# One attention layer's edges: the first batch's expert sums divided anew between VectorE and GpSimd, the last batch's splits spread over rounds, its last projections and statistics reordered

## The chip, the cores and the metric

The kernel runs on one core of a Trainium2 chip. The metric is the device time of one execution in microseconds (us), lower is better. TensorE is called PE, VectorE DVE, ScalarE ACT and GpSimd POOL, as in the profile.

## The reference, cut to what matters

Two transformer layers with a layer norm behind every sublayer, on x of 8 batches x 512 tokens x 512 features, all in fp32:

```python
x = L0_attn_x
x = _layernorm(x + _L0_attn_ref(x, ...))   # 16 heads, causal
x = _layernorm(x + _L0_ffn_ref(x, ...))    # 8 experts, the 2 best of each token, weighted
x = _layernorm(x + _L1_attn_ref(x, ...))   # 8 query heads on 2 key/value heads
x = _layernorm(x + _L1_ffn_ref(x, ...))    # integer weights times a scale, SiLU-gated
```

The change lies in the third line and at its borders. In short, that line is

```python
def _L1_attn_ref(x, norm_scale, split_scale, Wq, Wk, Wv, Wo):
    nrm = jnp.linalg.norm(x, axis=-1, keepdims=True) * d ** (-0.5)
    h = norm_scale * x / (nrm + EPS) * split_scale
    q, k, v = h @ Wq.T, h @ Wk.T, h @ Wv.T          # by heads
    attn = softmax(q k / sqrt(64)); out = attn v
    return x + out @ Wo.T
```

## The kernel before, in words

The 512 tokens of a batch b are held as `xs[b]`, 128 partitions x 4 row blocks (t = 0 to 3) x 512 features. Layer 1's attention (`Attention1`) runs over the 8 batches in turn. Within a batch there are 4 head pairs g, and for each pair 4 key blocks kt: 16 units. A round i of 8 takes two units, so that an even round has kt 0 and 1 of a pair and an odd round kt 2 and 3. In `batches`, a round issues, in this order:

- `score` of its two units: two matmuls each on PE ("sc", two tiles of two PSUM banks each), and the exponential on ACT (L1582) into one of four buffers "p";
- `add` (L1590) of the units of the round before, on DVE: the running "total" over key blocks, one addition after an even round, two after an odd one;
- the round's further pieces of work, from the list `todo[i]` that `plan` (L1616) makes;
- `product` (L1601) of the units of the round before, on PE ("av"), and, when these ended a head pair, `normalise` (L1606): the row sums "rs" on PE (L1609) from the total, their copy to SBUF on ACT (L931), the reciprocal on DVE (L1612), the product with "av" into "aoT" on DVE (L1613), and a running sum for a later validity test on POOL (L934).

The further pieces are: `query` (L1498), the projection of the next head pair's queries; `project` (L1544), the output projection of one row block of the batch before (`project_groups`, one matmul for each of the 4 head pairs) with `residual` (L1554), which adds x on DVE (L1557) and takes the statistics of the layer norm (L1561, L1562; for the last row block also two small POOL operations, L1565 and L1566); `norm` (L1568), which applies it; and the preparation of the next batch. That preparation (`Combine`, L655) gathers the two expert results of each row block from DRAM by indirect DMA on POOL's queue (`fetch`, L673, eight gathers "yr"), adds them to x with their weights, either on DVE with two fused operations (`add`, L680, then `stat`) or on POOL with four operations (`sum`, L689 and L690, with `stat` issued separately), takes statistics on DVE (`stat`, L694, L695), computes deviations on POOL (L701 to L703), norms on DVE (L710 to L714, "xn"), and turns the result with PE (`turn`, L1477) for `key`, `value` and `query`. In batch 0 the preparation is that of batch 1, and its gathers begin with the stage, since the gathered rows are then complete; POOL does the sums of three row blocks, DVE those of one. In the other batches DVE does all four.

In the last batch there is no next batch to prepare. Instead it makes the input of layer 1's feed-forward part for batch 0: `split` (L1012), for each of 4 feature blocks c, turns x on PE into a PSUM tile "ps_xT" (L1022), rounds it on ACT to "x_high" (L1023) and takes the remainder on DVE as "x_low" (L1024).

After the last round the last total, products and row sums follow, then the output projection of batch 7 into four PSUM tiles `banks`, and its statistics. Then `IntegerFfn.run` (L1026) begins: for each batch 11 chunks c of the hidden width. A chunk's gate and up matmuls (L1055, "ps_g" and "ps_u") are followed by SiLU on ACT (L1058), a product on DVE (L1060, "hT"), its rounding on ACT (L1063) and its remainder on DVE (L1064). The down matmuls (L1069, "ps_f") of a chunk come after the gate and up matmuls of the next. Weights come as integers by DMA from SP's queue into one slot (L980), are converted on DVE (L994), and their largest magnitude is watched on DVE (L926) for the validity test.

What sets the order: in layer 1's attention, PE, DVE, ACT and POOL run their instructions in the order of the code (`in_order`, L1523), each engine waiting where an input is missing. In the feed-forward part the framework's planner orders the instructions by its own estimate of when each is ready, with the order of the code as priority; low-priority ones fill gaps. PSUM has 8 banks: in the attention, two for the tag "mm" (queries, projections, splits, row sums), four for "sc" and two for "av". A tile of a tag takes a buffer that is free, and waits for one if none is. The feed-forward part opens its own PSUM tiles over all of them, and its first matmul waits for the last readers of the banks that it takes.

Of the kernel before, what the change touches and what calls it, by code (L numbers as in the profile page):

```python
# [18 lines left out]
P = 128  # L19
NB = 8  # L20
S = 512
D = 512
NT = S // P
ND = D // P
# [48 lines left out]
class Env:  # L73
# [19 lines left out]
    def open_stream(self, ctx, batches, **kw):  # L93

        resident = ctx.enter_context(self.tc.tile_pool(name=f"resident{batches[0]}", bufs=1, **kw))
        for b in batches:
            self.xs[b] = resident.tile([P, NT, D], F32, tag=f"x{b}", name=f"x_{b}")
# [904 lines left out]
class IntegerFfn:  # L1002
# [9 lines left out]
    def split(self, b, c, ps):  # L1012


        nc = self.nc
        if c == 0:
            pool = self.work if b % 2 else self.rows
            self.halves[b] = [pool.tile([P, ND, S], F32R, tag=f"rows{i}", name=f"x3_{part}")
                              for i, part in enumerate(("high", "low"))]
        high, low = self.halves[b]  # L1020
        for t in range(NT):
            nc.tensor.transpose(ps[:, ts(t, P)], self.env.xs[b][:, t, ts(c, P)], self.env.ident)  # L1022
        nc.scalar.copy(high[:, c, :], ps)  # L1023
        nc.vector.tensor_tensor(low[:, c, :], ps, high[:, c, :].bitcast(F32), ALU.subtract)  # L1024
# [420 lines left out]
class Attention1:  # L1445
# [80 lines left out]
    def batches(self, work, p_sc, p_av, weights, split):  # L1526
        env, nc, guard, state, HD = self.env, self.nc, self.guard, self.state, self.HD
        xs = env.xs
# [15 lines left out]
        def project(b, t):  # L1544
            ps = self.mm([P, D], "ps_o1")
            project_groups(b, t, ps, range(ND))
            residual(b, t, ps)

        def project_groups(b, t, ps, groups):
            for c in groups:  # L1550
                nc.tensor.matmul(ps, lhsT=state[b]["aoT"][:, c, ts(t, P)], rhs=w_out[:, c, :],  # L1551
                                 start=c == 0, stop=c == ND - 1)

        def residual(b, t, ps):  # L1554
            st = state[b]
            x = xs[b][:, t, :]
            nc.vector.scalar_tensor_tensor(x, x, st["scale"][t], ps, ALU.mult, ALU.add)  # L1557
            if t == 0:
                st["stats"] = small.tile([P, NT, 6], F32, name="stats1")
                st["mv"] = small.tile([P, NT, 2], F32, name="mv1")  # L1560
            nc.vector.bn_stats(out=st["stats"][:, t, :], in_=x)  # L1561
            nc.vector.bn_aggr(out=st["mv"][:, t, :], in_=st["stats"][:, t, :])  # L1562
            if t == NT - 1:
                st["rstd"] = rstd = small.tile([P, NT], F32, name="rstd1")
                nc.gpsimd.tensor_scalar(rstd, st["mv"][:, :, 1], LN_EPS, None, ALU.add)  # L1565
                nc.gpsimd.tensor_tensor(rstd, rstd, env.neg_half, ALU.pow)  # L1566

        def norm(b):  # L1568
            st = state.pop(b)
            for t in range(NT):  # L1570
                x = xs[b][:, t, :]
                nc.vector.tensor_scalar(x, x, st["mv"][:, t, 0:1], st["rstd"][:, t : t + 1], ALU.subtract, ALU.mult)
# [21 lines left out]
        def product(b, g, kt, p):  # L1594
            st = state[b]
            if b and (g, kt) == (0, 0):
                st["aoT"] = work.tile([P, ND, S], F32, tag="aoT", name="aoT1", bufs=2)
            if kt == 0:
                st["av"] = p_av.tile([P, S], F32, tag="av", name="av1")
            for j in range(2):  # L1600
                nc.tensor.matmul(st["av"][HD * j : HD * (j + 1), :], lhsT=st["v"][:, kt, HD * j : HD * (j + 1)],  # L1601
                                 rhs=p[:, j, :], start=kt == 0, stop=kt == NT - 1)
            if kt == NT - 1:
                return lambda total=st["total"], av=st["av"]: normalise(b, g, total, av)
# [11 lines left out]
        def plan(b):  # L1616


            todo = [[] for _ in range(ND * NT // 2)]
            here = pieces.pop(b)  # L1620
            first, final = b == 0, b == NB - 1
            then = None if final else self.prepare(b + 1)
            if not final:
                pieces[b + 1] = then
                todo[0] += [lambda t=t: then["fetch"](t) for t in range(NT)]
            for g, i in zip((1, 2, 3), (1, 3, 5) if first else (0, 1, 5) if final else (0, 1, 3)):
                todo[i].append(lambda g=g: here["query"](g))
            if b:
                for t, i in enumerate((2, 3, 4, 7) if final else (2, 3, 4, 5)):
                    todo[i].append(lambda t=t: project(b - 1, t))  # L1630
                if not final:
                    todo[6].append(lambda: norm(b - 1))
            if final:
                for c, i in enumerate((4, 6, 6, 6)):
                    todo[i].append(lambda c=c: split(0, c, self.mm([P, S], "ps_xT")))
            else:
                if first:

                    for t, i in ((1, 1), (2, 2), (3, 3)):
                        todo[i].append(lambda t=t: then["sum"](t))  # L1640
                        todo[i + 1].append(lambda t=t: then["stat"](t))
                for t, i in ((0, 2),) if first else ((0, 2), (1, 2), (2, 3), (3, 4)):
                    todo[i].append(lambda t=t: then["add"](t))
                todo[4].append(then["deviations"])

                todo[5].insert(0, then["norm"])
                todo[6] += [lambda c=c: then["turn"](c) for c in range(ND)]
                todo[6].append(then["key"])
                todo[7] += [then["value"], lambda: then["query"](0)]
            for i in (7,) if first else (1, 7):  # L1650
                todo[i] += [weights.convert, lambda: weights.load(work, 2, weights.FIRST)]
            return todo

        last = []
        for b in range(NB):
            for i, thunks in enumerate(plan(b)):
# [6 lines left out]
                sums = [product(*unit) for unit in last]  # L1663
# [3 lines left out]
        for unit in last:  # L1667
            add(*unit)
        sums = [product(*unit) for unit in last]
        sums[-1]()  # L1670

        b = NB - 1
        banks = [self.mm([P, D], "ps_o1") for _ in range(2)]
        banks += [p_sc.tile([P, 2, S], F32, tag="sc", name="ps_o1")[:, 0, :] for _ in range(2)]
        for t in range(NT):
            project_groups(b, t, banks[t], range(ND - 1))
        norm(b - 1)
        for t in range(NT):
            project_groups(b, t, banks[t], (ND - 1,))
            residual(b, t, banks[t])  # L1680
        return lambda: norm(b)


# [346 lines left out]
```

## Time and profile before

| | us |
|---|---|
| three runs | 2298.08, 2293.88, 2297.77 |
| median | 2297.77 |
| profiled execution, time | 2295.71 |
| profiled execution, span of its instructions | 2293.9 |
| PE busy | 2240.5 (98%) |
| DVE busy | 1245.0 (54%) |
| ACT busy | 648.2 (28%) |
| POOL busy | 501.6 (22%) |
| layer 1's attention, first score to last projection | 1189.5 to 1772.3 |

Times inside the kernel are counted from the start of the span. The span is about 1.8 us shorter than the time of the same execution, and the profiled execution lies between the lowest and the highest of the three runs. In the profile a matmul of 512 columns in fp32 appears as two records, and ends of matmuls are modelled, so records overlap slightly.

### The profile page before, as it was taken

The page shows a single profiled execution, that of the slowest core. Times are in us where ns is not written, and L with a number is a line of the kernel's source. Part 1 is how long each engine was busy: PE and PEld are TensorE (multiplying, and loading weights), DVE is VectorE, ACT ScalarE, POOL GpSimd, SP SyncE. Part 2 cuts the span into 40 slices and gives each one's busy share as a digit, 9 for nine tenths or more (in the row PEclk, how much of TensorE's full clock was granted, in tenths as well). Part 3 has the DMA queues.
Part 4 walks back from the last instruction along what each step waited for, and adds up shares of the span by engine and source line. Part 5 has one row for each costly group of instructions (what it writes and reads, how often), then busy time and mean ns, then how long its engine had stood idle before and what let it go on. Part 6 is the DMA issues. An engine that isn't in the chain of part 4 may idle for free.

```text
span 2293.9 us, 24187 instructions
## 1 busy us (share of the span) xinstructions
PE 2240.5 (98%) x9430; PEld 1154.8 (50%) x9430; DVE 1245.0 (54%) x1974; ACT 648.2 (28%) x937; POOL 501.6 (22%) x493
## 2 busy tenths in 40 slices
PE   9999999999999999999998999999998999999997
PEld 3344444444444444444443334443343878888876
DVE  3457575666668432242216877777667544444443
ACT  2332323323324221111223323333332322222222
POOL 2231323413224231131125122321211000000000
PEclk9999999999999999999999999999999999999999
DMA  8010110101112234332233011100100100000000
GB/s 289 19 56 1 55 33 23 56 7 49 54 38 84 92 115 146 93 120 91 87 127 94 10 55 56 55 29 17 37 1 23 42 19 19 19 19 19 19 19 20
DMA packets 58444, 126.63 MB, mean 55 GB/s; under 512 B 6210, under 2 KB 6210, under 8 KB 58322
## 3 DMA queue, kind: packets, MB, share of 16 engines
q1 hardware_dynamic: 47040, 89.32, 11.1%
q0 software_dynamic: 10560, 34.61, 5.2%
q8 instruction: 77, 1.26, 0.2%
q10 hardware_dynamic: 722, 1.07, 0.1%
q14 instruction: 45, 0.37, 0.1%
HBM read 89.59 MB, written 35.39 MB: 54 GB/s over the span
## 4 chain that ended last, share of the span: by engine, by line
PE 76%; issue 8%; DVE 7%; DMA 4%; POOL 4%; ACT 2%; POOLq 0%; SPq 0%; ACTq 0%; DVEq 0%
PE ps_f L1069 7%; PE ps_g L1055 6%; PE ps_u L1055 6%; PE ps_gu L845 5%; PE ps_o L1216 5%; PE ps_o L1551 5%; PE av L1601 5%; PE sc L1579 4%; PE ps_q L1503 4%; PE ps_q L1200 4%; PE ps_k L1208 4%; PE ps_v L1193 4%; PE av L1288 3%; PE sc L1264 3%; PE ps_y L862 2%
## 5 line engine op out<-in xcount | busy, mean ns | idle before, releaser
L845 PE MATMUL ps_gu<-experts,xrT 128*128 128x512 f32 (+1 forms) x520 | 248.6, 601 | 0.0
L1268 ACT ACTIVATE p<-sc 128x2048 f32<-128x2048 f32 (+1 forms) x96 | 152.9, 1593 | 189.0 <-PE sc L1264 182.1
L1273 POOL TENSOR_SCALAR_AFFINE_SELECT p<-p 128x512 f32<-128x512 f32 x128 | 92.1, 734 | 380.1 <-ACT p L1268 376.6
L1060 DVE SCALAR_TENSOR_TENSOR hT<-ps_u,vec,sg 128x512 f32<-128x512 f32 x88 | 65.8, 748 | 201.4 <-PE ps_u L1055 201.4
L1069 PE MATMUL ps_f<-ffn_w,h_half 128*128 128x512 f32 x672 | 169.4, 392 | 1.1 <-DVE h_half L1064 1.1
L934 POOL TENSOR_TENSOR g_total<-g_total,r_inv 128x512 f32<-128x512 f32 x64 | 89.7, 1402 | 361.4 <-DVE r_inv L1612 286.2
L1612 DVE RECIPROCAL r_inv<-r_inv 128x512 f32<-128x512 f32 x32 | 106.8, 3339 | 105.4 <-ACT r_inv L931 105.4
L1582 ACT ACTIVATE p<-sc 128x1024 f32<-128x1024 f32 x128 | 124.1, 1021 | 130.3 <-PE sc L1579 119.7
L1296 DVE TENSOR_TENSOR p<-p 128x1536 f32<-128x1536 f32 (+2 forms) x96 | 129.3, 1346 | 38.5 <-POOL p L1273 21.5
L1055 PE MATMUL ps_g<-x_high,ffn_w 128*128 128x512 f32 x352 | 141.5, 402 | 3.0 <-DVE x L1557 3.0
L1069 PEld LDWEIGHTS ps_f<-ffn_w,h_half 128*128 128x128 f32 x672 | 124.5, 188 | 33.7 <-DVE h_half L1064 7.2
L848 DVE TENSOR_TENSOR h<-ps_gu,h 128x256 f32<-128x256 f32 x67 | 28.4, 424 | 205.2 <-ACT h L847 205.2
L1055 PE MATMUL ps_g<-x_low,ffn_w 128*128 128x512 f32 x352 | 139.4, 396 | 0.0
L1055 PE MATMUL ps_u<-x_high,ffn_w 128*128 128x512 f32 x352 | 139.2, 395 | 0.0
L1055 PE MATMUL ps_u<-x_low,ffn_w 128*128 128x512 f32 x352 | 139.2, 395 | 0.0
L1579 PE MATMUL sc<-qT,kT 64*128 64x512 f32 x512 | 127.9, 618 | 1.0 <-ACT qT L1505 0.7
L862 PE MATMUL ps_y<-experts,hT 128*128 128x512 f32 (+1 forms) x272 | 127.9, 592 | 0.5 <-ACT hT L856 0.5
L1200 PE MATMUL ps_q<-experts 128*128 128x512 f32 x256 | 120.4, 611 | 4.4 <-DMA experts<-in_xT 4.4
L845 PEld LDWEIGHTS ps_gu<-experts,xrT 128*128 128x128 f32 x520 | 89.6, 192 | 68.0 <-issue 68.0
L1601 PE MATMUL av<-p,v 128*64 128x512 f32 x512 | 123.8, 605 | 0.0
L1193 PE MATMUL ps_v<-experts 128*128 128x512 f32 x256 | 116.3, 602 | 2.4 <-DVE v L1195 2.4
L1208 PE MATMUL ps_k<-experts 128*128 128x512 f32 x256 | 117.5, 602 | 0.2 <-ACT r_inv L931 0.2
(256 smaller groups left out, 3544.5 us busy)
## 6 DMA issues: line engine op xcount, KB each, us to landing
results<-y SPq DMA_DIRECT2D x68, 256.0 KB
x<-in_x SPq DMA_DIRECT2D x8, 1024.0 KB
experts<-in_gate_up SPq DMA_DIRECT2D x8, 1024.0 KB
rows<-x SPq DMA_DIRECT2D x32, 256.0 KB
x<-rows SPq DMA_DIRECT2D x8, 1024.0 KB
experts<-in_xT SPq DMA_DIRECT2D x7, 1024.0 KB
out<-x SPq DMA_DIRECT2D x28, 256.0 KB
ffn_i<-in_wq_ffn SPq DMA_DIRECT2D x11, 512.0 KB
```

The source lines that it names most:

```text
L845: mm = nc.tensor.matmul(ps, lhsT=xT[:, c, :], rhs=self.weights(i, c), start=c == 0, stop=c == ND - 1)
L862: self.nc.tensor.matmul(ps, lhsT=hT[:, c, :], rhs=self.weights(i, ND + c), start=c == 0, stop=c == self.NI - 1)
L1055: nc.tensor.matmul(ps, lhsT=w[:, ts(dc, P)], rhs=x[:, dc, :], start=(dc, i) == (0, 0), stop=(dc, i) == (ND - 1, 1))
L1069: self.nc.tensor.matmul(os[t], lhsT=h[:, ts(t, P)], rhs=self.weights(2 * NHID + c), start=(c, i) == (0, 0), stop=(c, i) == (NHID - 1, 1))
L1193: nc.tensor.matmul(ps, lhsT=xts[b][:, c, ts(t, P)], rhs=wv[:, c, :], start=c == 0, stop=c == ND - 1)
L1200: nc.tensor.matmul(ps, lhsT=wq[:, g, ts(c, P)], rhs=xts[b][:, c, :], start=c == 0, stop=c == ND - 1)
L1208: nc.tensor.matmul(ps, lhsT=wk[:, g, ts(c, P)], rhs=xts[b][:, c, :], start=c == 0, stop=c == ND - 1)
L1268: nc.scalar.activation(p, sc[:, :, :width], AF.Exp, scale=scale)
L1296: nc.vector.tensor_tensor(total[:, :, P * kt :], total[:, :, P * kt :], p[:, :, at : at + w], ALU.add)
L1579: nc.tensor.matmul(sc[:, j, :], lhsT=st["kT"][hs, ts(kt, P)], rhs=st["qT"][g][hs, :], start=True, stop=True)
L1582: nc.scalar.activation(p, sc, AF.Exp, scale=scale)
L1601: nc.tensor.matmul(st["av"][HD * j : HD * (j + 1), :], lhsT=st["v"][:, kt, HD * j : HD * (j + 1)], rhs=p[:, j, :], start=kt == 0, stop=kt ...
```

## The change

There are four edits.

1. In batch 0, POOL sums row blocks 2 and 3 (in rounds 1 and 2, their statistics on DVE two rounds later instead of one) and DVE adds row blocks 0 and 1 (in rounds 1 and 2). Before, POOL summed 1, 2 and 3 (rounds 1, 2 and 3) and DVE added block 0 in round 2. The gathers keep their order.
2. In the last batch the four splits are issued in rounds 0, 2, 4 and 6 instead of 4, 6, 6 and 6.
3. After the last round, the projection of row block 0 of batch 7 into the first bank, for three of the four head pairs, is issued ahead of the last row sums. The second bank is taken after them.
4. `statistics` is a function of its own. `project` still calls it right behind `residual`; at the end of the last batch the four residuals are issued first and the four row blocks' statistics behind them.

```diff
@@ project
             residual(b, t, ps)
+            statistics(b, t)
...
             nc.vector.scalar_tensor_tensor(x, x, st["scale"][t], ps, ALU.mult, ALU.add)
+
+        def statistics(b, t):
+            st = state[b]
+            x = xs[b][:, t, :]
             if t == 0:
...
@@ plan
             if final:
-                for c, i in enumerate((4, 6, 6, 6)):
+                for c, i in enumerate((0, 2, 4, 6)):
                     todo[i].append(lambda c=c: split(0, c, self.mm([P, S], "ps_xT")))
             else:
                 if first:
-                    for t, i in ((1, 1), (2, 2), (3, 3)):
+                    for t, i in ((2, 1), (3, 2)):
                         todo[i].append(lambda t=t: then["sum"](t))
-                        todo[i + 1].append(lambda t=t: then["stat"](t))
-                for t, i in ((0, 2),) if first else ((0, 2), (1, 2), (2, 3), (3, 4)):
+                        todo[i + 2].append(lambda t=t: then["stat"](t))
+                for t, i in ((0, 1), (1, 2)) if first else ((0, 2), (1, 2), (2, 3), (3, 4)):
                     todo[i].append(lambda t=t: then["add"](t))
                 todo[4].append(then["deviations"])
...
@@ batches, after the last round
         sums = [product(*unit) for unit in last]
+
+        b = NB - 1
+        banks = [self.mm([P, D], "ps_o1")]
+        project_groups(b, 0, banks[0], range(ND - 1))
         sums[-1]()
-
-        b = NB - 1
-        banks = [self.mm([P, D], "ps_o1") for _ in range(2)]
+        banks.append(self.mm([P, D], "ps_o1"))
         banks += [p_sc.tile([P, 2, S], F32, tag="sc", name="ps_o1")[:, 0, :] for _ in range(2)]
-        for t in range(NT):
+        for t in range(1, NT):
             project_groups(b, t, banks[t], range(ND - 1))
         norm(b - 1)
         for t in range(NT):
             project_groups(b, t, banks[t], (ND - 1,))
             residual(b, t, banks[t])
+        for t in range(NT):
+            statistics(b, t)
         return lambda: norm(b)
```

## The prediction

> **What bounds the kernel now.** I read the page first, then the timelines of PE, DVE and POOL through the layer-1 attention (1187 to 1786 us), then the busy time and granted clock in 1 us stretches around each gap of PE.
>
> ```profile
> PE 2240.5 (98%) x9430; PEld 1154.8 (50%) x9430; DVE 1245.0 (54%) x1974; ACT 648.2 (28%) x937; POOL 501.6 (22%) x493
> ```
>
> PE is busy 98% of the span, so the time is PE's work plus its gaps. Its timeline has four large gaps in this stage, and each touches the change. First batch, rounds 2 to 5 (start, length, engine, work, [idle before <- releaser]):
>
> ```profile
> 1202.99 1.03 PE L1609 MATMUL rs<-total,ones 128*64 128x512 f32 x4
> ...
> 1213.28 1.94 PE L1601 MATMUL av<-p,v 128*64 128x512 f32 x8
> 1220.09 1.97 PE L1609 MATMUL rs<-total,ones 128*64 128x512 f32 x4 [4.87 <-DVE total L1590]
> ```
>
> The row sums of head pair 1 (rs) start 4.87 us after PE was free, on DVE's total. DVE's timeline says why that total is late:
>
> ```profile
> 1205.88 0.69 DVE L694 BATCH_NORM_STATS2 stats<-x 128x6 f32<-128x512 f32 x1 [9.26 <-POOL x L690]
> ...
> 1206.70 2.58 DVE L680 SCALAR_TENSOR_TENSOR x<-yr,r_weights,x 128x512 f32<-128x512 f32 x2
> ...
> 1216.64 3.39 DVE L1590 TENSOR_TENSOR total<-total,p 128x1024 f32<-128x1024 f32 x2
> ```
>
> DVE stood 9.26 us waiting for GpSimd's first sum; recip, the next totals and rs stood behind it. The idle also halves the clock (each stretch: length, busy time of PE, PEld, DVE, ACT and POOL, then PEclk, DMA share, GB/s):
>
> ```profile
> 1220.00:1221.00 1.00, 0.91 (x3) 0.29 (x4) 0.04 (x1) 0.00 (x0) 1.00 (x1) 0.50 0.00 0
> ...
> 1222.00:1223.00 1.00, 1.00 (x4) 0.50 (x4) 0.15 (x1) 0.69 (x2) 0.82 (x1) 0.50 0.00 0
> ```
>
> From rs to the next products PE needs 8.13 us (1220.09 to 1228.22); the same steps take 6.5 later (1333.06 to 1339.57), so the half clock costs 1.6.
>
> Last batch and the border to the next layer:
>
> ```profile
> 1743.06 0.66 PE L1022 MATMUL ps_xT<-ident,x 128*128 128x128 f32 x4 [1.41 <-DVE x_low L1024]
> ...
> 1757.24 1.08 PE L1609 MATMUL rs<-total,ones 128*64 128x512 f32 x4 [1.67 <-DVE total L1590]
> 1758.25 14.00 PE L1551 MATMUL ps_o<-attn_out,aoT 128*128 128x512 f32 x32
> 1775.25 0.50 PE L1055 MATMUL ps_g<-x_high,ffn_w 128*128 128x512 f32 x1 [3.00 <-DVE x L1557]
> ```
>
> 1.41 us wait for a split's bank, 1.67 for the last total, then 3.00 for the last residual (L1557), after which the clock is 0.50 again:
>
> ```profile
> 1778.00:1779.00 1.00, 1.00 (x4) 0.81 (x3) 1.00 (x3) 0.73 (x1) 0.00 (x0) 0.50 0.00 0
> ```
>
> The first 16 gate/up matmuls take 5.38 us (1775.25 to 1780.63), the next 16 take 3.73: 1.65 lost.
>
> **The change, part by part.** All work stays: per row block the same adds, statistics and matmuls. What moves is order and engine.
>
> *First batch.* GpSimd loses block 1 (two pairs of 1.56 + 1.27, 5.7 us alone) and begins with block 2 in round 1; DVE gains two L680 operations. In round 1 add(0) makes DVE wait for a gather, with round 2's totals, and behind them rs of head pair 0, queued. The trace's DMA records end the second gather at 1198.3. Then, on DVE: second L680 0.74 and statistics 0.85 to 1200.0; two totals 2.56 (free) to 3.0 (partly beside GpSimd) to 1202.6-1203.0, while PE comes to rs at 1202.99: nothing lost. add(1) beside GpSimd 2.58 + 0.85 to 1206.2; recip 3.32 and product 0.77 to 1210.3; total 1.74 to 1212.0; statistics of block 2 0.85 to 1212.8; two totals 3.39 beside GpSimd, 2.54 free, to 1215.4-1216.2. PE is free at 1215.22, so of 4.87 us about 1.0 stays; with all free durations 0, with GpSimd's slowest pairs 1.5. GpSimd has block 2 from 1201.5 (fourth-last gather) to some 1209 and block 3 to 1216 at its slow rows (2.53 + 1.54), early enough for the statistics in rounds 3 and 4 and the deviations (2.2 us) before the norm in round 5. xn then ends 9.9 us after rs starts and PE asks for it 10.3 after. An idle of 1.0 should not drop the clock, since 1.67 did not (0.50 appears only after 4.87 and 3.00). Gain 4.87 - 1.0 + 1.6 = 5.5 (4.9 to 6.5).
>
> The Trainium skill (TensorE: Matmul & The Clock Gate, Part 1) says the clock halves after at least one idle window of about 3.4 us. By that the 3.00 us gap would cost no clock, and the sum below would be 1.65 smaller; the trace's 0.50 at 1776 to 1780 speaks against so strict a reading.
>
> *Splits.* One per round 0, 2, 4, 6 instead of three in round 6. Each is 0.5 us of PE, 0.59 of ACT, 0.66 of DVE, and DVE idles 10.8 us before 1700.30 and 1.8 before 1715.99. With one split in round 4 the trace shows no PE gap (1727.97, then products at 1728.50). Gain 1.4; if the cover failed, at most 0.7 for each moved one.
>
> *Last sums.* Three groups of block 0 (6 records of 0.43, 2.6 us) go ahead of rs, over the 1.67 gap. But the pair of "mm" banks is then held by block 0 and rs, so block 1 needs the bank of rs, free only after ACT has read it: rs ends 1758.3, ACT's read 1759.1, a new wait of 0.85 (bounds 0.7 and 1.0). Block 3's recip and product come 0.9 later, still 3 us before the last groups. Gain 1.67 - 0.85 = 0.8.
>
> *Residuals before statistics.* Now each residual (0.73) waits behind 0.87 of statistics of the block before; the fourth ends 2.94 after PE's last projection. With the residuals alone DVE keeps up with PE (0.86 per block) and the fourth ends 0.85 after it. Gain 2.1, and with an idle of 0.9 no half clock: 1.65 more (0 to 1.65; the drop need not be in every run).
>
> *What is late next.* The first down matmul (L1069 at 1784.36) needs DVE work that stood behind the statistics:
>
> ```profile
> 1774.48 0.71 DVE L1557 SCALAR_TENSOR_TENSOR x<-x,dev,ps_o 128x512 f32<-128x512 f32 x1
> ...
> 1775.96 0.18 DVE L1562 BATCH_NORM_AGGREGATE mv<-stats 128x2 f32<-128x6 f32 x1
> 1777.62 1.00 DVE L1572 TENSOR_SCALAR x<-x,mv,rstd 128x512 f32<-128x512 f32 x2 [1.48 <-POOL rstd L1566]
> 1778.53 1.22 DVE L994 TENSOR_SCALAR ffn_w<-ffn_i 128x2048 fp32r<-128x2048 int32 x1
> ...
> 1780.13 2.28 DVE L926 TENSOR_REDUCE g_widest<-ffn_w 128x1 f32<-128x2048 f32 x1
> 1782.33 0.74 DVE L1060 SCALAR_TENSOR_TENSOR hT<-ps_u,vec,sg 128x512 f32<-128x512 f32 x1
> ...
> 1783.92 0.69 DVE L1064 TENSOR_TENSOR h_half<-hT,h_half 128x512 fp32r<-128x512 f32 x1 [0.40 <-ACT h_half L1063]
> ```
>
> L1064 ended 1784.61, just in time. Count from the end D of the projection. Statistics now end at D + 4.15 (before D + 3.9), while PE reaches L1069 at D + 0.9 + 2 x 3.73 = D + 8.4 (before D + 12.1). The order here isn't fixed by hand but by the planner. If the urgent ones go first: weights land 4.8 to 5.4 after D, L994 to D + 6.2, hT to 6.95, ACT 0.62, L1064 to 8.3: nothing lost. If one watch (L926, 2.28) comes between: 2 lost. If the old order stays: L1064 at D + 12.7, about 4 lost, and such an idle halves the clock, 1.65 more. The planner takes what is ready, and hT is ready 2.7 us earlier against the statistics, so I take 1.5, bounds 0 and 5.5.
>
> Sum: 5.5 + 1.4 + 0.8 + 2.1 + 1.65 - 1.5 = 10.0 us. The profiled execution took 2295.71 (span 2293.9 and 1.8 around it), giving 2285.7; the median of the runs, 2297.77, lies 2.1 above it, giving 2287.8. I say 2287.
>
> **Rivals.**
> A (forecast, 0.58): as above, 2287; own range 2283 to 2290.
>
> B (0.24): the border gives its gain back. The planner leaves norms and watches ahead of hT; L1064 comes at D + 12.7. For it: DVE is busy without a break from 1777.62 to 1789.2. Against: the operations ahead have no reader close by. The last two parts then shrink to 0.5, less 1.65 of clock: 5.5 + 1.4 + 0.5 - 1.65 = 5.8, time 2291 (2290 to 2292).
>
> C (0.08): contention keeps the first gap. With DVE's two-input operations beside GpSimd at twice their free time (totals 2.56 to 5.1, total 1.24 to 2.5, add 1.51 to 3.0, and 1.0 in the totals of round 2) the chain is up to 3.9 longer; rs comes near 1219.5 and the clock drops: gain 0.6 instead of 5.5, time 2292.7. The rows stand against the factor of 2 for totals (3.39 to 2.56 is 1.3) and nearer it for L680, 1.29 each there, beside this mean of later batches:
>
> ```profile
> L680 DVE SCALAR_TENSOR_TENSOR x<-yr,r_weights,x 128x512 f32<-128x512 f32 x48 | 35.3, 736 | 0.9
> ```
>
> This is the rule of the Trainium skill (GPSIMD Engine Reference, 8. Key points) that GpSimd shares its SBUF interfaces with VectorE and contends with instructions of two SBUF inputs; it speaks against giving DVE more such work here, and the rows bear it out in part.
>
> D (slower, 0.05): DVE now waits in order for the first gathers. Those 2 MB share the DMA engines with 5.5 MB of rows and weights until 1213. rs of pair 1 follows the second landing by 16.8 us, so, with the half clock after so long an idle, a landing after 1203.3 undoes the first part and one after 1207.8 makes the whole slower; served behind the bulk (1211), rs comes at 1228, 7.7 later in effect than before: 2301. Against: the records show both sharing from 1195 on, and GpSimd started block 1 at 1199.99 without a wait.
>
> Other, 0.05: the later layer's automatic order shifts by small amounts either way.
>
> About 0.2% (4.6 us) is what a measurement can tell. Faster: A, nearly all of B and most of C, 0.86. Same: rests of B and C and others, 0.08. Slower: D and a rest, 0.06. Range 2283 (all gains, from the profiled time) to 2294 (B from the median with the first part at 4.9 and half of the splits' gain is 2293.3; B and C together, 2297, I leave out).
>
> **What would show it.** Right: rs of pair 1 starting before 1217 with no 0.50 clock after it; no gap at the splits in round 6; a 0.7 to 1.0 wait on ACT's read behind the last rs; the first L1055 within 1 us of the last projection at full clock; PE waits of under 2.5 us at the first L1069. Wrong: an idle of over 2.5 us before rs, a DVE wait on a gather with PE waiting for round 2's totals, or L1064 of chunk 0 more than 11 us after the projection's end.

## The result and the profile after

| | before | after |
|---|---|---|
| median of five runs, us | 2297.77 | 2284.40 |
| lowest and highest, us | 2293.88, 2301.07 | 2282.12, 2287.36 |
| profiled execution, time and span, us | 2295.71, 2293.9 | 2286.21, 2284.5 |

The kernel is faster: the ratio is 0.9944, with a 95% interval of 0.993 to 0.9959, that is 9.4 to 16.1 us. The forecast was 2287, in a range of 2283 to 2294. In the code after, the lines from `project` (L1544) on have moved: the total is L1595, "av" L1606, "rs" L1614, the reciprocal L1617, the projection L1552, the last residual L1558, the statistics L1566 and L1567, the norm L1577. The feed-forward lines (L1055 to L1069, L994, L926) are the same.

The page's first part shows the same work in less time; DVE has two more instructions and POOL four fewer, the sums of block 1.

```profile
PE 2238.4 (98%) x9430; PEld 1153.0 (50%) x9430; DVE 1242.0 (54%) x1976; ACT 648.2 (28%) x937; POOL 496.2 (22%) x489
```

PE's timeline in the first batch (start, length, engine, line, work, and in brackets the idle before it):

```profile
1205.55 1.08 PE L1614 MATMUL rs<-total,ones 128*64 128x512 f32 x4
...
1215.90 1.94 PE L1606 MATMUL av<-p,v 128*64 128x512 f32 x8
1217.66 1.03 PE L1614 MATMUL rs<-total,ones 128*64 128x512 f32 x4
1218.62 1.99 PE L1584 MATMUL sc<-qT,kT 64*128 64x512 f32 x8
1220.54 3.70 PE L1503 MATMUL ps_q<-hT,attn_qkv 128*128 128x512 f32 x8
1224.17 1.94 PE L1606 MATMUL av<-p,v 128*64 128x512 f32 x8
```

The wait of 4.87 us ahead of the row sums of head pair 1 is gone altogether: "rs" follows "av" without a bracket, and the next products come 6.51 us after it (1217.66 to 1224.17) instead of 8.13. DVE's timeline of the same stretch says how the total came in time:

```profile
1200.18 0.75 DVE L680 SCALAR_TENSOR_TENSOR x<-yr,r_weights,x 128x512 f32<-128x512 f32 x1 [3.80 <-DMA yr<-results,r_results_i]
1201.27 0.75 DVE L680 SCALAR_TENSOR_TENSOR x<-yr,r_weights,x 128x512 f32<-128x512 f32 x1 [0.34 <-DMA yr<-results,r_results_i]
...
1202.89 2.52 DVE L1595 TENSOR_TENSOR total<-total,p 128x1024 f32<-128x1024 f32 x2
1205.33 1.97 DVE L680 SCALAR_TENSOR_TENSOR x<-yr,r_weights,x 128x512 f32<-128x512 f32 x2
...
1212.17 1.22 DVE L1595 TENSOR_TENSOR total<-p,p 128x1024 f32<-128x1024 f32 x1
...
1214.12 3.10 DVE L1595 TENSOR_TENSOR total<-total,p 128x1024 f32<-128x1024 f32 x2
1218.42 0.69 DVE L694 BATCH_NORM_STATS2 stats<-x 128x6 f32<-128x512 f32 x1 [1.19 <-POOL x L690]
```

The waits on gathers (3.80 and 0.34) and on POOL's last sum (1.19) are there, but the first two end before PE asks for its row sums, and the last stands behind the totals, which end at 1217.22, 0.4 before PE is free. Busy time of the engines (PE, PEld, DVE, ACT, POOL), then the granted clock, show no 0.50 where it was 0.50 before:

```profile
1218.00:1219.00 1.00, 1.00 (x6) 0.30 (x4) 0.58 (x1) 0.00 (x0) 1.00 (x2) 1.00 0.06 16
...
1768.00:1769.00 1.00, 1.00 (x6) 0.77 (x5) 0.93 (x4) 0.00 (x0) 0.00 (x0) 1.00 0.88 307
```

PE's timeline at the end of the last batch and at the border:

```profile
1737.38 0.66 PE L1022 MATMUL ps_xT<-ident,x 128*128 128x128 f32 x4
...
1752.59 1.08 PE L1614 MATMUL rs<-total,ones 128*64 128x512 f32 x4
1754.51 11.43 PE L1552 MATMUL ps_o<-attn_out,aoT 128*128 128x512 f32 x26 [0.84 <-ACT r_inv L931]
1766.78 0.50 PE L1055 MATMUL ps_g<-x_high,ffn_w 128*128 128x512 f32 x1 [0.84 <-DVE x L1558]
...
1774.95 1.17 PE L1069 MATMUL ps_f<-ffn_w,h_half 128*128 128x512 f32 x4 [0.45 <-issue]
...
1777.05 1.19 PE L1069 MATMUL ps_f<-ffn_w,h_half 128*128 128x512 f32 x4
```

No split waits. The waits of 1.67 and 3.00 have become 0.84 (on ACT's read of the row sums) and 0.84 (on the last residual). The only new loss is at the first down matmuls (L1069).

The stages below carry the rest of the text. Each is a difference of two starts in PE's timeline, so it is free of what happens ahead of the change. That matters, because the first score of the attention, which lies ahead of all four edits, started between 1186.7 and 1192.6 in the profiles of this study.

| stage, us | before | after |
|---|---|---|
| first score to "rs" of pair 0 | 13.49 | 13.63 |
| first score to "rs" of pair 1 | 30.59 | 25.74 |
| that "rs" to the next products | 8.13 | 6.51 |
| last batch: first score to the last products | 60.79 | 59.16 |
| last products to the end of the projection | 20.33 | 19.69 |
| to the first L1055 | 3.00 | 0.84 |
| first 16 gate and up matmuls | 5.38 | 3.83 |
| from there to the first turning for the next batch (ps_xT) | 11.13 | 12.08 |
| from there to the end of the span | 502.14 | 501.80 |
| first score of the attention to the end | 1104.40 | 1092.57 |

### The profile page after: what moved, and what is told of

The parts are those of the page before. It is cut to its first block, busy times and chain, and to the rows that moved or that the text cites. A ratio compares the mean times of both kernels' runs of the same rounds, so it can differ in the third digit from the quotient of the medians.

```text
span 2284.5 us, 24183 instructions
## 1 busy us (share of the span) xinstructions
PE 2238.4 (98%) x9430; PEld 1153.0 (50%) x9430; DVE 1242.0 (54%) x1976; ACT 648.2 (28%) x937; POOL 496.2 (22%) x489
## 5 line engine op out<-in xcount | busy, mean ns | idle before, releaser
L1069 PE MATMUL ps_f<-ffn_w,h_half 128*128 128x512 f32 x672 | 169.8, 393 | 1.6 <-DVE h_half L1064 1.1
L1617 DVE RECIPROCAL r_inv<-r_inv 128x512 f32<-128x512 f32 x32 | 106.9, 3339 | 97.5 <-ACT r_inv L931 97.5
L1069 PEld LDWEIGHTS ps_f<-ffn_w,h_half 128*128 128x128 f32 x672 | 124.3, 188 | 34.9 <-DVE h_half L1064 7.6
L1055 PE MATMUL ps_g<-x_high,ffn_w 128*128 128x512 f32 x352 | 141.0, 401 | 0.8 <-DVE x L1558 0.8
L1055 PE MATMUL ps_g<-x_low,ffn_w 128*128 128x512 f32 x352 | 139.0, 395 | 0.0
L1055 PE MATMUL ps_u<-x_low,ffn_w 128*128 128x512 f32 x352 | 138.8, 394 | 0.0
L1055 PE MATMUL ps_u<-x_high,ffn_w 128*128 128x512 f32 x352 | 138.6, 394 | 0.0
L1606 PE MATMUL av<-p,v 128*64 128x512 f32 x512 | 123.7, 605 | 0.0
L1552 PE MATMUL ps_o<-attn_out,aoT 128*128 128x512 f32 x256 | 117.3, 602 | 0.8 <-ACT r_inv L931 0.8
```

The costliest lines, as they stand in the source:

```text
L1055: nc.tensor.matmul(ps, lhsT=w[:, ts(dc, P)], rhs=x[:, dc, :], start=(dc, i) == (0, 0), stop=(dc, i) == (ND - 1, 1))
L1069: self.nc.tensor.matmul(os[t], lhsT=h[:, ts(t, P)], rhs=self.weights(2 * NHID + c), start=(c, i) == (0, 0), stop=(c, i) == (NHID - 1, 1))
```

## The experiments

My theory was that the four edits act at four separate places with the sums forecast. The rivals of it were that something else than the totals' chain stood ahead of the first gap, that the clock was not the gaps' doing, and that the planner's order at the border, not the residuals, decided what the last edit brings. All ratios are against the kernel before, run beside the experiment on the same chip.

**One edit at a time.** First the new division of the sums alone:

```diff
-                    for t, i in ((1, 1), (2, 2), (3, 3)):
+                    for t, i in ((2, 1), (3, 2)):
                         todo[i].append(lambda t=t: then["sum"](t))
-                        todo[i + 1].append(lambda t=t: then["stat"](t))
+                        todo[i + 2].append(lambda t=t: then["stat"](t))
-                for t, i in ((0, 2),) if first else ((0, 2), (1, 2), (2, 3), (3, 4)):
+                for t, i in ((0, 1), (1, 2)) if first else ((0, 2), (1, 2), (2, 3), (3, 4)):
```

> Only the first batch's sums are divided anew. Theory (PE's gaps vanish one by one, each with its own worth): rs of head pair 1 starts about 25.7 us after the first score instead of 30.6, the clock stays at 1.00 there and the next steps take 6.5 instead of 8.1: 6.5 us less; the gaps of 1.41, 1.67 and 3.00 in the last batch stay. Rival (the gaps are one chain, and what is won early is lost at the border to the next layer): the time falls by less than 3 us, and the last gaps grow.

Measured: 2290.41 (2287.01 to 2291.31), ratio 0.9961 [0.9947, 0.9975]. The row sums of pair 1 start 25.55 after the first score and the next products 6.51 after them: 5.04 + 1.62 = 6.7 us, all of the first batch's gain. PE's timeline of this kernel (lines as before the change) has no wait there:

```profile
1216.33 1.94 PE L1601 MATMUL av<-p,v 128*64 128x512 f32 x8
1218.10 1.03 PE L1609 MATMUL rs<-total,ones 128*64 128x512 f32 x4
```

The splits alone:

```diff
-                for c, i in enumerate((4, 6, 6, 6)):
+                for c, i in enumerate((0, 2, 4, 6)):
```

> Only the splits are spread. Theory: the 1.41 us gap in round 6 of the last batch goes and nothing takes its place: 1.4 to 1.6 us less, all between the last batch's first score and its last products. Rival (the splits of rounds 0 and 2 cost elsewhere, in ACT's or DVE's queue ahead of the row sums): under 0.7 less, with new PE waits on ACT or DVE in rounds 0 to 3.

Measured: 2296.28 (2289.76 to 2298.57), ratio 0.9987 [0.9976, 0.9998]. The stage up to the last products is 59.16 instead of 60.79: 1.63, as in the whole change. In its profiled execution the border took most of it back: the same gap of 2.99 was followed by two windows of half clock instead of one. The last section shows what decides between one and two.

```profile
1776.00:1777.00 1.00, 0.43 (x1) 0.43 (x2) 0.97 (x2) 0.00 (x0) 0.00 (x0) 0.50 1.04 401
...
1781.00:1782.00 1.00, 1.00 (x4) 0.80 (x3) 1.00 (x3) 0.99 (x2) 0.00 (x0) 0.50 0.00 0
1782.00:1783.00 1.00, 1.00 (x5) 0.79 (x4) 1.00 (x1) 0.48 (x1) 0.00 (x0) 0.68 0.48 76
```

The clock is 0.50 from before 1776 to past 1782, and the first 16 gate and up matmuls take 6.57 us here, 1.2 more than the 5.38 before.

The last sums alone:

```diff
-        sums[-1]()
...
-        banks = [self.mm([P, D], "ps_o1") for _ in range(2)]
+        banks = [self.mm([P, D], "ps_o1")]
+        project_groups(b, 0, banks[0], range(ND - 1))
+        sums[-1]()
+        banks.append(self.mm([P, D], "ps_o1"))
...
-        for t in range(NT):
+        for t in range(1, NT):
             project_groups(b, t, banks[t], range(ND - 1))
```

> Only the fill ahead of the last row sums. Theory: the 1.67 us gap goes, a wait of 0.84 on ACT's read of the row sums comes: 0.6 to 0.8 less up to the last projection; the 3.00 us gap behind it stays, and whether the clock halves there is open: total 0.6 to 2.3 less. Rival (the three groups cover the gap at no price): 1.67 less and no wait on ACT.

Measured: 2296.04 (2293.22 to 2301.07), ratio 0.9996 [0.9986, 1.0006]: by the runs it can't be told from no change. The stage says 19.70 instead of 20.33, a gain of 0.63, and PE's timeline shows the trade, the wait of 1.67 on DVE's total for one on ACT's read:

```profile
1758.54 1.08 PE L1609 MATMUL rs<-total,ones 128*64 128x512 f32 x4
1760.45 11.43 PE L1551 MATMUL ps_o<-attn_out,aoT 128*128 128x512 f32 x26 [0.84 <-ACT r_inv L931]
```

This profiled execution had two windows of half clock behind both large gaps (the steps behind the first take 9.07 us, the first 16 gate and up matmuls 6.60), so from the first score to the end it took 1105.46, longer than the kernel before, although its own stage is shorter.

The residuals ahead of the statistics alone (the `statistics` function, and at the end):

```diff
         for t in range(NT):
             project_groups(b, t, banks[t], (ND - 1,))
             residual(b, t, banks[t])
+        for t in range(NT):
+            statistics(b, t)
```

> Only the four residuals ahead of the four statistics at the end of the attention. Theory: the 3.00 us gap shrinks to 0.84, the clock stays at 1.00 (5.4 to 3.8 us for the first 16 gate and up matmuls), and about 1 us of it is lost again at the first down matmuls: 2.5 to 3 less. Rival (the border gives it all back, since the remainder of the hidden product on DVE is just in time before): under 1 us less, with PE waiting 3 us or more at the first down matmul.

Measured: 2295.54 (2288.93 to 2296.24), ratio 0.998 [0.9971, 0.9989]. PE's timeline has the short gap:

```profile
1775.16 0.50 PE L1055 MATMUL ps_g<-x_high,ffn_w 128*128 128x512 f32 x1 [0.84 <-DVE x L1558]
```

The gap falls by 2.16 (3.00 to 0.84), the first 16 matmuls by 1.53 (5.38 to 3.85), and the stretch to the first turning grows by 0.95 (11.13 to 12.08): 2.74 in sum. The planner's new order at the border, with its loss, belongs to this edit alone.

By stages the four gains are 6.66 + 1.63 + 0.63 + 2.74 = 11.66, and from the first score to the end the whole change gained 1104.40 - 1092.57 = 11.83. So the edits add up to within 0.2 us, and no interaction shows.

**What held the first gap.** In the kernel before, DVE stood 9.26 us waiting for POOL's sum of block 1 to take its statistics. Is it that one instruction's place in the queue, or the amount of POOL's work? This kernel only moves the statistics of block 1 one round on:

```diff
-                        todo[i + 1].append(lambda t=t: then["stat"](t))
+                        todo[3 if t == 1 else i + 1].append(lambda t=t: then["stat"](t))
```

> The old division (GpSimd sums blocks 1, 2 and 3), but the statistics of block 1 stand one round later, so that DVE no longer waits for GpSimd ahead of head pair 0's reciprocal. Theory (the amount of work on GpSimd counts too): rs of pair 1 loses its 4.87 us gap, but GpSimd's third sum still ends some 31 us after the first score, DVE waits for it ahead of pair 1's reciprocal, and PE waits 3 to 4.5 us at the turning of xn instead: 0.4 to 2.5 us less in all. Rival (only the place of the wait in DVE's queue counts): the whole 6.5 us, with no gap at the turning.

Measured: 2294.81 (2289.32 to 2297.73), ratio 0.9985 [0.9975, 0.9995]. The timelines of PE and of DVE:

```profile
1219.38 1.08 PE L1609 MATMUL rs<-total,ones 128*64 128x512 f32 x4 [1.85 <-DVE total L1590]
...
1230.92 4.44 PE L1477 MATMUL ps_hT<-ident,xn 128*128 128x128 f32 x16 [1.13 <-DVE xn L714]
```

```profile
1215.41 0.70 DVE L694 BATCH_NORM_STATS2 stats<-x 128x6 f32<-128x512 f32 x1 [2.00 <-POOL x L690]
...
1223.40 0.69 DVE L694 BATCH_NORM_STATS2 stats<-x 128x6 f32<-128x512 f32 x1 [4.07 <-POOL x L690]
```

Up to the row sums 3.0 us are won (27.57 instead of 30.59), the clock after them stays at 1.00, and so the next products come 6.56 later instead of 8.13. But POOL's three sums still end late: the statistics of block 2 wait 2.00, those of block 3 another 4.07, "xn" comes 1.13 after PE wants it, and the turning that follows, in part at half clock, takes 4.37 us to the key projection instead of 3.31. From the first score to the last products of the last batch this kernel gains 2.0 us (562.42 to 560.41), where the new division gains 6.7. That is within the 0.4 to 2.5 expected, though not at the places that I had named: 1.85 of the first gap stays, and the wait at the turning is 1.13 and not 3 to 4.5. The rest of the 6.7 needs the work itself to leave POOL.

**What the clock cost.** To part the gap from the clock, the kernel before was given five idle matmuls into an unused bank ahead of those row sums. They change no output.

```diff
                 if last and sums[-1]:
+                    if (b, i) == (0, 4):
+                        idle = self.mm([P, S], "ps_idle")
+                        for c in range(5):
+                            nc.tensor.matmul(idle, lhsT=state[0]["hT"][:, c % ND, :P], rhs=state[0]["hT"][:, c % ND, :],
+                                             start=c == 0, stop=c == 4)
                     sums[-1]()
```

> The kernel before with five matmuls more in the first gap, into a bank that nothing reads; they only keep PE busy for 4.3 of the 4.87 us, and rs still waits for DVE's total. Theory (the gap costs its length and, beyond it, a half clock): rs starts at the same distance from the first score, 30.6 us, the clock stays at 1.00, and the steps from rs to the next products take 6.5 us instead of 8.1: 1.6 us less. Rival (the slow steps come from something else, such as GpSimd's traffic): they still take 8.1 us, no gain.

Measured: 2296.01 (2291.43 to 2297.83), ratio 0.9993 [0.9985, 1.0002]; unclear by the runs. By PE's timeline "rs" starts as late as before (30.59 after the first score), yet the next products come 6.56 us later and not 8.13:

```profile
1212.39 4.56 PE L1668 MATMUL ps_idle<-hT 128*128 128x512 f32 x10
1217.32 1.08 PE L1609 MATMUL rs<-total,ones 128*64 128x512 f32 x4 [0.37 <-DVE total L1590]
1218.33 1.99 PE L1579 MATMUL sc<-qT,kT 64*128 64x512 f32 x8
1220.25 3.70 PE L1503 MATMUL ps_q<-hT,attn_qkv 128*128 128x512 f32 x8
1223.88 1.94 PE L1601 MATMUL av<-p,v 128*64 128x512 f32 x8
```

POOL does the same sums beside these steps as before, so its traffic isn't what made them slow. 1.57 of the 8.13 is the half clock that the idle brought; 0.55 of it is lost again at the turning (3.86 instead of 3.31), which starts earlier and now waits for DVE's "xn" block by block: its first eight transposes take 2.08 instead of 1.09.

```profile
1227.66 2.08 PE L1477 MATMUL ps_hT<-ident,xn 128*128 128x128 f32 x8
```

**What is left.** The 0.84 on ACT's read: here blocks 1 and 2 of the last projection take the free "sc" banks, and block 3 the bank of "rs", in the kernel after.

```diff
-        banks.append(self.mm([P, D], "ps_o1"))
         banks += [p_sc.tile([P, 2, S], F32, tag="sc", name="ps_o1")[:, 0, :] for _ in range(2)]
+        banks.append(self.mm([P, D], "ps_o1"))
```

> The kernel after, with the last projection's blocks 1 and 2 in the scores' banks and block 3 in the bank of the row sums. Theory (the 0.84 us wait is for that bank, until ACT has read it): the wait goes and the last projection ends 0.84 us earlier against the kernel after. Rival (block 1 waits for something else of ACT): the wait stays.

Measured: 2280.90 (2280.43 to 2284.83), ratio 0.9935 [0.9922, 0.9948]. The wait is gone, and the stage is 18.80 instead of 19.70:

```profile
1750.92 1.08 PE L1614 MATMUL rs<-total,ones 128*64 128x512 f32 x4
1751.93 11.43 PE L1552 MATMUL ps_o<-attn_out,aoT 128*128 128x512 f32 x26
```

The 0.95 at the first down matmuls: is it the watch (L926, 2.28 us on DVE)? In the kernel after, the watches on the last 13 weight blocks were moved behind the first batch in the code and cut into pieces of one block (a quarter of the largest), which needs a wider tile for their results:

```diff
-        self.widest = env.const.tile([P, 16], F32, name="g_widest")
+        self.widest = env.const.tile([P, 32], F32, name="g_widest")
...
-            self.guard.watch_integers(w.bitcast(F32))
+            if late is not None:
+                late += [w[:, i, :].bitcast(F32) for i in range(n)]
+            else:
+                self.guard.watch_integers(w.bitcast(F32))
...
                 if b == 0:
+                    for w in late:
+                        self.guard.watch_integers(w)
```

> The kernel after, with the watch on the last 13 weight blocks issued block by block (0.62 us each instead of up to 2.28) and later in the code. Theory (the watch of 2.28 us ahead of the first remainder is what the first down matmuls wait for): from the end of the first 16 gate and up matmuls to the first turning for the next batch 11.1 to 11.4 us instead of 12.1; 0.7 to 1 us less than the kernel after. Rival (the weights' arrival or ACT decides): 12.1 stays.

Measured: 2286.81 (2284.94 to 2287.91), ratio 0.9956 [0.9943, 0.9968]. The theory fell: the stage took 12.26 (12.08 after). PE's timeline shows why (L1075 is L1069 in this kernel): the first down matmuls still start with a wait, and the eight take 2.51.

```profile
1774.08 2.51 PE L1075 MATMUL ps_f<-ffn_w,h_half 128*128 128x512 f32 x8 [0.43 <-issue]
```

The wait ahead of them ends with the rounding of "hT" on ACT (1773.36 to 1773.98), ahead of which no watch stands. The wait among them is for the remainder, ahead of which the planner still put two pieces of the watch:

```profile
1773.24 1.27 DVE L926 TENSOR_REDUCE g_widest<-ffn_w 128x1 f32<-128x512 f32 x2
1774.43 0.68 DVE L1070 TENSOR_TENSOR h_half<-hT,h_half 128x512 fp32r<-128x512 f32 x1
```

So this run takes 1.0 us of watch from ahead of the remainder, not all of it, and gains nothing.

Besides, the 500 us behind it became 2.4 us longer (504.19 for 501.80). That could have been the smaller pieces or the wider tile. The tile alone, in the kernel after:

```diff
-        self.widest = env.const.tile([P, 16], F32, name="g_widest")
+        self.widest = env.const.tile([P, 32], F32, name="g_widest")
```

> The kernel after, with one thing changed: the tile that collects the watches has 32 columns instead of 16, of which the second half is unused. Theory (the watches in small pieces cost nothing by themselves; the wider tile moves every tile behind it in SBUF by 64 bytes a partition, and the down matmuls run slower from there): a group of 8 down matmuls takes 2.00 to 2.02 us as in the run with the pieces, and from the first turning to the end it is about 504 us instead of 502. Rival (the pieces or their place did it): 1.98 and 502.

Measured in a single execution: 2285.16, and 504.08 us to the end. So it is the wider tile. That it acts by putting later tiles 64 bytes further on in each partition is inferred from the code; no run shows it. The groups of the down matmuls, of the kernel after and of this one (count, busy time, mean ns of one, idle before):

```profile
L1069 PE MATMUL ps_f<-ffn_w,h_half 128*128 128x512 f32 x672 | 169.8, 393 | 1.6 <-DVE h_half L1064 1.1 <-issue 0.4
```

```profile
L1069 PE MATMUL ps_f<-ffn_w,h_half 128*128 128x512 f32 x672 | 171.9, 396 | 1.4 <-DVE h_half L1064 1.0 <-issue 0.4
```

The same 672 records take 2.1 us more. Why wasn't tried.

The other reason for the 0.95 could be DVE's norms, which stand ahead of "hT". In the kernel with the new banks, the last batch's four norms were given to POOL:

```diff
-        return lambda: norm(b)
+        def last_norm():
+            st = state.pop(b)
+            for t in range(NT):
+                x = xs[b][:, t, :]
+                nc.gpsimd.tensor_scalar(x, x, st["mv"][:, t, 0:1], st["rstd"][:, t : t + 1], ALU.subtract, ALU.mult)
+
+        return last_norm
```

> The kernel after, with the other order of banks of the run before and with the last batch's norm (four operations) on GpSimd instead of DVE. Theory (what the first down matmuls wait for is DVE standing 1.48 us for GpSimd's rstd and doing two norms ahead of the first hidden product): that wait and 2.1 us of norms leave DVE's queue, the first remainder comes 2 us or more earlier, and from the end of the first 16 gate and up matmuls to the first turning for the next batch it takes 11.1 to 11.4 us instead of 12.1: 0.7 to 1 less, and with the banks' 0.9 some 1.7 less than the kernel after. Rival (the weights' arrival or the planner's order of PE decides): 12.1 stays, 0.9 less by the banks alone.

Measured: 2285.06 (2281.82 to 2287.18), ratio 0.9944 [0.9931, 0.9958]. DVE's timeline has "hT" right behind ACT, 1.2 us after the last statistics, with the remainder (L1064) 2.15 after its start and the watch behind both; PE's has the eight down matmuls together and without a wait:

```profile
1770.32 0.75 DVE L1060 SCALAR_TENSOR_TENSOR hT<-ps_u,vec,sg 128x512 f32<-128x512 f32 x1 [1.16 <-ACT sg L1058]
1770.98 1.57 DVE L994 TENSOR_SCALAR ffn_w<-ffn_i 128x2048 fp32r<-128x2048 int32 x1
1772.47 0.68 DVE L1064 TENSOR_TENSOR h_half<-hT,h_half 128x512 fp32r<-128x512 f32 x1
1773.08 2.27 DVE L926 TENSOR_REDUCE g_widest<-ffn_w 128x1 f32<-128x2048 f32 x1
```

```profile
1773.59 1.98 PE L1069 MATMUL ps_f<-ffn_w,h_half 128*128 128x512 f32 x8
```

The stage is 11.09 (12.08 after, 11.13 before), so the 0.95 goes when the norms and the wait for their "rstd" no longer stand ahead of "hT" on DVE. The planner also put the watch behind the remainder here, so the run doesn't part the two; but the run with the smaller watch shows that this alone gains nothing. From the first score to the end this kernel has the least of all, 1090.97, against 1091.75 with the new banks alone and 1092.57 after. The kernel after ran once more beside it:

> The kernel after once more, beside the others on one chip. Expected: the same stage times as in its first profile to 0.1 us, apart from what lies ahead of the first score, and a ratio to the kernel before of 0.993 to 0.996.

Measured: 2283.49 (2279.93 to 2285.55), ratio 0.9938 [0.9925, 0.9951], with stages within 0.15 us of the first time (0.1 had been expected; the two starts of "rs" are 0.13 and 0.15 earlier), though its first score started at 1190.05 and not at 1191.92. So of the versions that go beyond the change none is shown faster than it by the runs: 0.9935 and 0.9944 against 0.9944 and 0.9938. A gain of 0.9 or 1.6 us, read from the stages, is smaller than what moves ahead of them from run to run.

## Why the prediction was right, step by step

| step | forecast, us | measured by stages, us |
|---|---|---|
| first batch: gap and clock | 4.87 - 1.0 + 1.6 = 5.5 (4.9 to 6.5) | 4.85 + 1.62 = 6.5 |
| splits | 1.4 | 1.63 |
| last sums | 0.8 | 0.63 |
| gap at the last residual | 2.1 | 2.16 |
| clock behind it | 1.65 | 1.55 |
| first down matmuls | -1.5 (0 to -5.5) | -0.95 |
| rest | 0 | 0.3 |
| sum | 10.0 | 11.8 |

The places and the signs were right. The likeliest case (A) came, and nothing was found late that the prediction had not named. Two sizes were off to the cautious side by 0.5 us or more, the first batch and the first down matmuls. The row "rest" is the stretch behind the border (502.14 to 501.80), which takes 501.7 to 502.3 in all profiles without the wider tile, so 0.3 there means nothing.

*First batch.* The term that was mis-sized is the remaining wait of 1.0; it was 0. The start of the chain was well placed: add(1) began at 1205.33, and the forecast's 1202.8 becomes 1205.2 with the first score 2.4 later. But I had given the operations beside GpSimd the durations of the slowest rows. The pair of L680 took 1.97 and not 2.58, the first total 1.22 and not 1.74, the two totals 3.10 and not 3.39: 1.4 us less, so that the totals end 0.4 before PE is free and not 1.0 after. POOL began block 2 at 1204.28, near the 1201.5 forecast (1203.9 in this count), and worked without a break beside all of these operations; yet the first total took no longer than its free duration, and the same L689 took POOL 1.56 at one time and 2.57 at another. What decides how much one engine slows the other isn't shown. The bound with all durations free (wait 0) was in the range, so the forecast was right about the chain and cautious about its rows. "xn" ended 10.8 after "rs" started, not 9.9, at no cost: the steps of the turning take 3.31 as before. Here the Trainium skill (GPSIMD Engine Reference, 8. Key points) says that GpSimd shares its SBUF interfaces with VectorE, with contention where a VectorE instruction has two SBUF inputs. The trace agrees for this pair (1.97, against 1.50 at 1200 to 1202, where POOL only issues gathers), but gives much less than the factor of 2 that rival C needed.

*Clock.* "An idle of 1.0 should not drop the clock" held: no window near the change is at 0.50 in the kernel after, nor behind the 0.84 gaps of the other experiments. The idle matmuls show the cause in the first batch. At the border it follows from the residuals' experiment, where the wait and the half clock go together. That the size fits so well (1.55 for 1.65) is in part luck: the 1.65 was read from one execution, and the same gap cost 1.3 to 2.8 in other profiles (last section).

*Splits.* 1.63 for 1.4. The wait in round 6 was 1.41. The other 0.2 comes from the two splits that left round 6: there they took 1.09 (the eight records ahead of the wait), while in rounds 0 and 2 each makes the time from the start of the projection ahead of it to the next products only 0.43 longer (3.63 to 4.06). Their cover in rounds 0, 2 and 4 held.

*Last sums.* The new wait is 0.84, as read from the end of "rs" to ACT's read (0.85). The gain is 0.63 and not 0.8, because the projection in two parts takes 2.77 + 11.43 where it took 14.00 in one. The new order of banks shows that the 0.84 was the price of the bank and could be avoided.

*Border.* The gap left is 0.84 (forecast 0.85). For the first down matmuls the forecast gave two marks, and they disagreed: it said that L1064 later than 11 us after the projection would be wrong, and L1064 ended 11.05 after it (1765.94 to 1776.99). Yet PE lost only 0.95. DVE's timeline after:

```profile
1771.40 1.00 DVE L1577 TENSOR_SCALAR x<-x,mv,rstd 128x512 f32<-128x512 f32 x2 [1.48 <-POOL rstd L1571]
1772.32 1.22 DVE L994 TENSOR_SCALAR ffn_w<-ffn_i 128x2048 fp32r<-128x2048 int32 x1
1773.45 0.75 DVE L1060 SCALAR_TENSOR_TENSOR hT<-ps_u,vec,sg 128x512 f32<-128x512 f32 x1
1774.11 2.28 DVE L926 TENSOR_REDUCE g_widest<-ffn_w 128x1 f32<-128x2048 f32 x1
1776.31 0.68 DVE L1064 TENSOR_TENSOR h_half<-hT,h_half 128x512 fp32r<-128x512 f32 x1
```

Two norms and a watch do stand ahead of the remainder, as rival B had it (though DVE was not quite without a break in the kernel before, as B said: it idled 0.40 at 1783.5). What B left out, and so did the forecast's count of 2 for a watch in between, is that the planner orders PE too: it issued the four down matmuls that need only the rounded part (1774.95), then four gate matmuls of the next chunk, and only then the four that need the remainder (1777.05). So the late remainder cost less than its lateness, since PE had other matmuls to fill with. The first half of the loss, 0.45, is the rounded part itself: "hT" behind the norms ends at 1774.20, its rounding on ACT at 1774.85. That the planner chose this order was not derived: 1.5 was a choice between bounds of 0 and 5.5, and that 0.95 came, not 4, is luck within them.

*Rivals C and D.* C's factor did not appear. D's wait did (3.80 us of DVE on the first gather), but the second gather landed by 1201.27, 4.4 us ahead of the point from which it would have undone the gain, and "rs" of pair 0 came only 0.14 later. That the change loses its gain elsewhere is excluded by the last rows of the table of stages.

*The number.* By stages the gain is 11.8. The profiled executions differ by 9.5 and the medians by 13.4; the difference of the former is smaller since the first score of this profiled execution came 2.4 later. The forecast's 2287 is the 10.0 taken from the median, with a part of the way to the profiled execution's time; the 1.8 that the steps missed explain most of its distance to 2284.4. The medians' 13.4 holds 1.6 more than the stages show, within the interval of 9.4 to 16.1; where it arises isn't shown.

## What to carry to other kernels

When an engine that runs in program order waits for another, moving the waiting instruction may only move the wait: here it won 2.0 of 6.7 us, and taking work off the late engine won all of it. A gap on PE is worth more than its length: here gaps of 3.0 and 4.9 us cost 1.3 to 2.8 us more in half clock, and gaps of 0.84 cost nothing beyond themselves, so the first look belongs to the gaps of two to three microseconds and more. A change of a few microseconds is read from stages that begin behind the last thing that varies by itself, since the medians here could hardly tell gains of 0.6 to 1.6 us.

## What the runs showed of the hardware that was not expected

The same gap of 3.0 us brought one window of half clock in some executions (3.4 us; first 16 matmuls 5.14 to 5.38) and two in others (6.8 us; 6.57 to 6.60), at full clock 3.83. The two windows in the clock records of the kernel before are 3.413 us long and start 556.373 apart, which is 163.0 times that length, as of a grid that runs freely. The Trainium skill (TensorE: Matmul & The Clock Gate, Part 1) gives a free-running window of 3413 ns, and the trace agrees. That it takes at least one idle window does not: at the border of the kernel before, the window ahead of the half clock was 1772.95 to 1776.36 (from the clock records; the mean clock of 0.68 between 1776 and 1777 agrees), and PE was idle for the first 2.3 us of it and busy for the rest.

What decides between one window and two can be read off by laying this grid over PE's timeline in all 13 profiles, from 860 to 2230 us. Each window of half clock that followed full clock had ahead of it a window with 1.96 us or more of idle PE, with one exception, and full-clock windows that were followed by full clock held 1.78 at most. A second window of half clock followed where PE was still idle for 0.71 us or more within the first (0.71, 0.75 and 1.62), and none did where it was idle for 0.51 or less. So the price of a gap depends on how the grid cuts it: the border's gap lay as 0.70 + 2.30 before the half clock in the kernel before, and as 2.24 before and 0.75 behind its start with the splits alone. Even an idle of 1.95 to 1.97 cost a window in two profiles, the new division alone and the new order of banks, where it fell into one window whole (L854, some 200 us ahead of the attention). These bounds were read after the fact, and no run was made to test them.

The exception is the kernel with the late statistics: the window ahead of its half clock (1229.17 to 1232.59) held 1.12 of idle and otherwise scores and 128x128 transposes. The idle of 1.85 in the same profile, which brought none, was cut by the grid into 1.41 and 0.44. Whether transposes count for less than other matmuls stayed open.

A tile that grew by 64 bytes per partition made the down matmuls behind it slower, 396 ns for 393, and the last 500 us 2.3 us longer (504.08 for 501.80, and 504.19 in the other kernel with that tile). The edit changes no instruction's place in the code.
